# Selective-scan kernel: the gating product issued one scan later at group borders, and a fourth buffer for quads of C

## The chip, the cores and the metric

The kernel runs on one core of a Trainium2 chip. The metric is the device time of one execution in microseconds (us); the time of a kernel is the median of several runs. One execution was also taken by the hardware profiler, and the views shown below are of that execution.

The core's engines are named as the profile names them: PE (TensorE, with PEld for its weight loads), DVE (VectorE), ACT (ScalarE), POOL (GpSimd) and SP (SyncE, which here only issues DMAs). Each engine works its own instructions strictly in the order in which the program issued them; engines wait for each other on semaphores.

## The reference

An image batch `x` of shape (2, 96, 128, 128) goes through two layers. Layer 0 has the work that matters here, four selective scans ("mamba") over the 16384 positions of an image, one for each direction of reading it:

```python
def step(h, t):
    dt_t, u_t, B_t, C_t = t
    dA = jnp.exp(dt_t[:, :, None] * A)
    h = dA * h + dt_t[:, :, None] * B_t[:, None, :] * u_t[:, :, None]
    y = jnp.einsum('bds,bs->bd', h, C_t)
    return (h, y)
...
y = ys.transpose(1, 0, 2) + Dp * xc
y = y * jax.nn.silu(z)
return y @ outp_w.T
```

There are 192 inner channels a direction and 16 states a channel. `xc`, `z`, `dt`, `B` and `C` come from small projections of the normalized input. After the four scans come a fused projection with a residual, a quantized feed-forward layer, a 3x3 convolution and a second feed-forward layer. Everything is float32 outside the feed-forward layers.

## The kernel before

For each of the two images there are three stages: `normalize` (L155), `mamba` (L185) and `ffn_and_conv` (L492). Only `mamba` is touched.

**Steps, groups, units.** Two directions are computed together, and their 2 x 192 channels fill three groups of 128 partitions (`g` = 0, 1, 2). A pair of directions takes 32 steps of T = 512 positions. There are two pairs an image, so 64 steps an image and 128 in all. Within a step the work is cut into 24 units: a unit is a group and two of its 16 states, `units = [(g, s) ...]` (L384). In this text a unit is named by its place in the step, 0 to 23; units 0 to 7 are group 0, 8 to 15 group 1, 16 to 23 group 2. Groups begin at units 0, 8 and 16.

**What a unit costs each engine.**
- SP fetches B and C. Both lie in DRAM as rows, and `row_tile` (L329) broadcasts a quad (four states, two units) over the partitions: one DMA of 1024 KB. The quads of B go round `B_AHEAD + 1` = 4 buffers, the quads of C round `C_AHEAD + 1` = 3.
- POOL multiplies a quad of B by dt*u in place (`b_part`, L339, 128x2048), then adds what the states carry over from the step before (L342, L343).
- ACT makes the decay exp(dt*A) into PSUM (`decay`, L349, two of 128x512). There are three such PSUM buffers.
- DVE runs the recurrence (`scan`, L353), two scans of 512 positions, and then multiplies the result by C in place of C (L441, 128x1024). For the units in `BY_POOL`, which are 0, 4, 8, 12, 16 and 20, POOL makes this product instead (`by_pool`, L360).
- ACT copies the last state aside (L442).
- PE sums the products over the states by matmuls with the identity (`sums`, L357) into the PSUM tile `y`. There is one `y` buffer. A group's `y` is opened by a matmul of the skip term (L448).

When a group is complete, DVE multiplies `y` by silu(z): the gate (`gated`, L364, 128x512). Only then can L448 of the next group open `y` again.

**Order.** `in_order` (L150) fixes the order in which every engine gets its instructions to the program's own. The loop at L469 goes over all units `k`: fetch B for unit k+6 and run `b_part` for unit k+2 (even k), prologue work of the next step that falls due (`issue(k, 0)`), first scan of unit k, then `behind(k - 1)`, the decay of unit k+2, the second scan of unit k, fetch of C for unit k+4 (even k), and the rest that falls due (`issue(k, 1)`). `behind(k - 1)` is what follows unit k-1's scans: the product with C, the copy of the state, at a group's begin the gate of the group before and L448, and the sums. Where POOL makes the product of unit k, it is issued in iteration k+1 and its sums on PE in iteration k+3.

So at a group's begin DVE gets: the first scan of unit k, the gate of the group that ended with unit k-2, the second scan of unit k. In a step these gates fall on iterations 9 (for group 0), 17 (for group 1) and 1 of the next step (for group 2).

**Prologue.** The next step's projections are spread over the units by `prologue` (L214) with a table of due times (L308 to L323): two convolutions of eight matmul pairs or matmuls at iterations 1, 5 and 9 (L211), z at 7, 18 and 21, rows of B and C at 12 (L266), dt at 14 to 16 (L284, L289), softplus at 17 (L293), dt*u on POOL at 19, 27 and 29 (L298). They share one PSUM tile, `misc`. The output projection of a group (`project`, L372 and L374) is due four units after its end and uses `misc` too.

**Buffers.** A DMA into a buffer waits on SP until the last reader of the old contents is done. For a quad of C the last reader is PE (L357); with a POOL unit in it that is three iterations after the unit.

Of the kernel before, what the change touches and what calls it, by code (L numbers as in the profile page):

```python
# [30 lines left out]
PAIRS = ((0, 2), (1, 3))  # L31
NG = 3
B_AHEAD = 3
C_AHEAD = 2
AHEAD = 2
BY_POOL = tuple((g, s) for g in range(3) for s in (0, 8))
BCO = 32
# [4 lines left out]
def tile_metaformer(ctx: ExitStack, tc: tile.TileContext, a: dict, out: bass.AP):  # L42
    nc = tc.nc
# [141 lines left out]
    def mamba(acc, xnr, xnc):  # L185

        with ExitStack() as st:
# [164 lines left out]
            def scan(j, da, b, h):  # L352
                nc.vector.tensor_tensor_scan(h[:, j, :], da[:, j, :], b[:, j, :], 0.0, ALU.mult, ALU.add)  # L353

            def sums(s, y, c):
                for j in range(2):
                    nc.tensor.matmul(y, ident, c[:, j, :], start=False, stop=s + j == S - 1)  # L357
# [4 lines left out]
            def gated(pi, d, g, y):  # L362
                t = d["sz"][:, g, :]
                nc.vector.tensor_tensor(t, y, t, ALU.mult)  # L364
                d["yg"].append(t[:, ::-1] if pi == 1 else t)
# [17 lines left out]
            steps = [(pi, i) for pi in range(2) for i in range(NT)]  # L383
            units = [(g, s) for g in range(NG) for s in range(0, S, 2)]  # L384
            nu = len(units)
            total = nu * len(steps)
            state = [{} for _ in steps]
            todo = {}

            def later(k, where, rank, f, *args):  # L390
                todo.setdefault((k, where), []).append((rank, partial(f, *args)))

            def issue(k, where):
                for _, f in sorted(todo.pop((k, where), ()), key=lambda p: p[0]):
                    f()
# [7 lines left out]
            def prepare(n):  # L403
                if n < len(steps):
                    for m, where, rank, f in prologue(*steps[n], state[n]):
                        k = (n - 1) * nu + m
                        if k < 0:
                            f()
                        else:
                            later(k, where, rank, f)  # L410
# [4 lines left out]
            def fetch(k, n, ahead, m):  # L415
                if k < total:
                    t = row_tile(state[k // nu], *units[k % nu], n, ahead)
                    m[k], m[k + 1] = t[:, 0:2, :], t[:, 2:4, :]
                    if n == 0:
                        quads[k] = t  # L420

            def feed(k):

                if k < total:
                    n = k // nu
                    b_part(steps[n][1], state[n], *units[k % nu], quads.pop(k))

            def feed_decay(k):
                if k < total:
                    n = k // nu  # L430
                    das[k] = decay(steps[n][0], state[n], *units[k % nu])

            ys = {}

            def behind(k):

                n, u = divmod(k, nu)
                (pi, i), d, (g, s) = steps[n], state[n], units[u]
                h, c = hs.pop(k), cs.pop(k)
                if (g, s) not in BY_POOL:  # L440
                    nc.vector.tensor_tensor(c, h, c, ALU.mult)  # L441
                nc.scalar.copy(hst[:, g, s : s + 2], h[:, :, T - 1])  # L442
                if s == 0:
                    if k > 0:
                        pn, pu = divmod(k - 1, nu)
                        gated(steps[pn][0], state[pn], units[pu][0], ys.pop(k - 1))
                    y = ps_y.tile([128, T], F32, name="y")
                    nc.tensor.matmul(y, dmat[:, pi, g, :], d["xc"][:, g, :], start=True, stop=False)  # L448
                else:
                    y = ys.pop(k - 1)  # L450
                ys[k] = y
                if (g, s) in BY_POOL:
                    later(k + 1, 1, True, by_pool, h, c)
                    later(k + 3, 1, True, sums, s, y, c)
                else:
                    sums(s, y, c)
                if k == total - 1:
                    gated(pi, d, g, y)
                if s == S - 2 and g > 0:
                    later(k + 4, 0, True, project, pi, i, d, g)  # L460
                    later(k + 5, 1, False, collect, pi, d, g)

            for m, (n, ahead) in ((bs, (0, B_AHEAD)), (cs, (1, C_AHEAD))):
                for k in range(ahead):
# [4 lines left out]
            for k in range(total + 6):  # L469
                n, u = divmod(k, nu)  # L470
                if u == nu - 3:

                    prepare(n + 2)
                if k % 2 == 0:
                    fetch(k + 2 * B_AHEAD, 0, B_AHEAD, bs)
                    feed(k + AHEAD)
                issue(k, 0)
                if k < total:
                    (g, s) = units[u]
                    da, b = das.pop(k), bs.pop(k)  # L480
                    hs[k] = b if (g, s) in BY_POOL else da
                    scan(0, da, b, hs[k])
                if 0 < k <= total:
                    behind(k - 1)
                feed_decay(k + AHEAD)
                if k < total:
                    scan(1, da, b, hs[k])
                if k % 2 == 0:
                    fetch(k + 2 * C_AHEAD, 1, C_AHEAD, cs)
                issue(k, 1)  # L490
# [101 lines left out]
    for b in range(NB):  # L592
        xnr = dpool.tile([C, L], F32, name="xnr")
        xnc = dpool.tile([C, L], F32, name="xnc")
        normalize(b, acc, xnr, xnc)
        mamba(acc, xnr, xnc)
        ffn_and_conv(b, acc)
# [71 lines left out]
```

## Time and profile before

| what | value |
|---|---|
| median of 3 runs | 11550.82 us |
| lowest to highest | 11549.54 to 11551.47 us |
| the profiled execution's own time | 11556.77 us |
| its span, first to last instruction | 11555.0 us |
| busy in the stretch 6100 to 10900 us (4800 us of `mamba`) | DVE 4639.98, POOL 4506.79, PE 4366.64, ACT 3387.67 us |
| DMA in that stretch | mean busy share 0.86 of 16 engines, 331 GB/s |
| TensorE's mean granted clock | 0.989 over the span, 1.00 in that stretch |

How to read it: the span is what lies between the first and last instruction, and the execution's own time is 1.8 us more. Busy is the time in which an engine executes; waits on semaphores are not in it. `mamba` is the two long stretches of the span, one for each image, some 500 to 5200 us and 6000 to 10950 us with their beginnings. A group's row in the profile ends with the idle time of its engine just before it and with who ended that idle time. In a timeline, a row gives start, duration, engine, line, and in brackets the idle time before it.

### The profile page before, as it was taken

How to read it: one execution, taken by the hardware profiler on the slowest of the kernel's cores; microseconds unless marked ns; L12 is line 12 of the kernel's file. 1: busy time of each engine (PE TensorE's matmuls, PEld its weight loads, DVE VectorE, ACT ScalarE, POOL GpSimd, SP SyncE). 2: the span in 40 equal slices, each digit the busy share in tenths (PEclk: the TensorE clock that was granted, in tenths of full speed). 3: DMA queues.
4: the chain of work that ended last, by engine and by line, in shares of the span. 5: the costliest groups of instructions: out<-in, count | busy, mean ns of one | idle time of the engine just before them, and what ended most of it. 6: DMA issues, size and time to landing. Idle time of an engine off the chain costs nothing. (4 is left out here: it accounts for less than half of the span.)

```text
span 11555.0 us, 94102 instructions
## 1 busy us (share of the span) xinstructions
PE 10435.0 (90%) x24208; PEld 3971.4 (34%) x24208; DVE 10421.6 (90%) x10127; ACT 7901.7 (68%) x13564; POOL 9672.3 (84%) x4700
## 2 busy tenths in 40 slices
PE   7999999999999999989989999999999999999899
PEld 2333333333333333333323333333333333333333
DVE  6999999999999999994469999999999999999944
ACT  6767767677677677665567677677676776776655
POOL 5999999999999999991159999999999999999911
PEclk8999999999999999999989999999999999999999
DMA  7888888888888888880068888888888888888800
GB/s 263 335 329 333 333 332 332 330 331 333 329 332 333 330 331 333 329 322 19 26 243 334 328 331 334 330 333 333 333 331 329 332 332 329 331 333 329 319 13 13
DMA packets 540755, 3416.96 MB, mean 296 GB/s; under 512 B 67532, under 2 KB 68652, under 8 KB 143832
## 3 DMA queue, kind: packets, MB, share of 16 engines
q1 hardware_dynamic: 539960, 3410.16, 76.8%
q8 instruction: 196, 3.21, 0.1%
q14 instruction: 343, 2.81, 0.1%
q0 software_dynamic: 256, 0.79, 0.0%
HBM read 3289.04 MB, written 54.53 MB: 289 GB/s over the span
## 5 line engine op out<-in xcount | busy, mean ns | idle before, releaser
L339 POOL TENSOR_TENSOR row<-dtu,row 128x2048 f32<-128x2048 f32 x1536 | 6948.9, 4524 | 283.3 <-DMA row<-bcd 281.6
L357 PE MATMUL y<-row,ident 128*128 128x512 f32 x12288 | 5690.6, 603 | 700.0 <-DVE row L441 699.9
L353 DVE TENSOR_TENSOR_SCAN da<-da,row 128x512 f32<-128x512 f32 x4608 | 5456.9, 1214 | 38.9 <-ACT da L349 5.2
L349 ACT ACTIVATE da<-dt,amat 128x512 f32<-128x512 f32 x6144 | 4246.9, 691 | 170.2
L357 PEld LDWEIGHTS y<-row,ident 128*128 128x128 f32 x12288 | 2256.8, 190 | 4008.4 <-issue 2243.5
L441 DVE TENSOR_TENSOR row<-da,row 128x1024 f32<-128x1024 f32 x2304 | 2776.7, 1205 | 70.2 <-DMA row<-bcd 70.0
L442 ACT COPY hst<-da 128x2 f32<-128x2 f32 x2304 | 368.9, 160 | 2652.2 <-DVE row L441 2649.3
L360 POOL TENSOR_TENSOR row<-row,row 128x1024 f32<-128x1024 f32 x768 | 1807.4, 2353 | 223.0 <-DVE row L353 147.5
L353 DVE TENSOR_TENSOR_SCAN row<-da,row 128x512 f32<-128x512 f32 x1536 | 1852.4, 1206 | 91.9 <-POOL row L339 84.1
L211 PE MATMUL misc<-xa,inx 96*64 96x512 f32 (+1 forms) x2048 | 946.1, 605 | 50.0 <-ACT mix L239 26.8
L211 PE MATMUL misc<-xb,inx 96*64 96x512 f32 (+1 forms) x2048 | 952.3, 608 | 33.6 <-ACT hst L442 24.2
L564 POOL TENSOR_TENSOR acc<-acc,y 96x512 f32<-96x512 f32 x128 | 147.4, 1151 | 991.5 <-DVE y L563 991.5
L298 POOL TENSOR_TENSOR dtu<-dt,xc 128x512 f32<-128x512 f32 x384 | 487.4, 1269 | 106.0 <-DMA xb<-xnc 99.8
L576 PE MATMUL pc<-pad,kw 96*96 96x512 f32 x1152 | 566.4, 593 | 0.0
L211 PEld LDWEIGHTS misc<-xa,inx 96*64 96x64 f32 (+1 forms) x2048 | 327.3, 165 | 581.2 <-issue 438.0
L448 PE MATMUL y<-xc,dmat 128*128 128x512 f32 x768 | 419.5, 628 | 103.6 <-DVE sz L364 103.6
L374 PE MATMUL misc<-sz,gmat 128*96 128x512 f32 x1024 | 484.1, 595 | 0.0
L284 PE MATMUL misc<-rows,dtw 12*128 12x512 f32 x768 | 434.3, 645 | 50.6 <-ACT dt L289 37.9
L364 DVE TENSOR_TENSOR sz<-y,sz 128x512 f32<-128x512 f32 x384 | 264.6, 689 | 229.5 <-PE y L357 198.0
L136 DVE TENSOR_TENSOR xq<-xm,rs 96x512 fp8e5<-96x512 f32 x128 | 87.9, 687 | 392.2 <-ACT rs L132 392.2
L211 PEld LDWEIGHTS misc<-xb,inx 96*64 96x64 f32 (+1 forms) x2048 | 316.5, 164 | 361.9 <-issue 214.1
L372 PE MATMUL misc<-acc,ident 96*96 96x512 f32 x512 | 387.6, 842 | 57.3 <-ACT sz L247 53.8
(76 smaller groups left out, 7449.9 us busy)
## 6 DMA issues: line engine op xcount, KB each, us to landing
row<-bcd SPq DMA_DIRECT2D x3072, 1024.0 KB, 7.4
xc<-mix SPq DMA_DIRECT2D x256, 128.0 KB, 5.4
sz<-mix SPq DMA_DIRECT2D x256, 128.0 KB, 8.9
xa<-xnr SPq DMA_DIRECT2D x124, 193.1 KB, 8.6
xb<-xnc SPq DMA_DIRECT2D x124, 193.1 KB, 8.7
bcd<-rows SPq DMA_DIRECT2D x128, 128.0 KB, 9.5
acc<-in_x_dram SPq DMA_DIRECT2D x16, 768.0 KB, 5.7
xnr<-xn SPq DMA_DIRECT2D x16, 768.0 KB, 4.3
```

The costliest lines, as they stand in the source:

```text
L211: nc.tensor.matmul(ps[rows, :], w(PAIRS[pi][d], k, lo, hi), src[d][:, k : k + T], **se)
L284: nc.tensor.matmul(d["ps"], w, d["rows"][0 : 2 * RK, :], start=True, stop=True)
L298: nc.gpsimd.tensor_tensor(dtu, d["dt"][:, g, :], d["xc"][:, g, :], ALU.mult)
L339: nc.gpsimd.tensor_tensor(b, d["dtu"][g][:, None, :].broadcast_to((128, 4, T)), b, ALU.mult)
L349: nc.scalar.activation(da[:, j, :], d["dt"][:, g, :], AF.Exp, scale=amat[:, pi, g, s + j : s + j + 1])
L353: nc.vector.tensor_tensor_scan(h[:, j, :], da[:, j, :], b[:, j, :], 0.0, ALU.mult, ALU.add)
L357: nc.tensor.matmul(y, ident, c[:, j, :], start=False, stop=s + j == S - 1)
L360: nc.gpsimd.tensor_tensor(c, h, c, ALU.mult)
L374: nc.tensor.matmul(d["po"], gmat[:, pi, 2 * g - 2 + k, :], d["yg"][g - 1 + k], start=False, stop=k == 1)
L441: nc.vector.tensor_tensor(c, h, c, ALU.mult)
L448: nc.tensor.matmul(y, dmat[:, pi, g, :], d["xc"][:, g, :], start=True, stop=False)
L576: nc.tensor.matmul(pc, kw[:, t, :], rows, start=t == 0, stop=t == 8)
```

## The change

Three edits.

1. `gate_before` holds the gate that stood in `behind`, and `begins(k)` tells whether unit k begins a group and has its product made by POOL (units 0, 8 and 16, which is every group's begin). Where unit k-1 begins a group, the whole of `behind(k - 1)` is issued after the second scan of unit k, not between its two scans. With it move the copy of the state on ACT (now behind the decay of unit k+2) and, on PE, the skip term's matmul L448; the order within PE, POOL and SP stays.
2. `C_AHEAD` goes from 2 to 3: C is fetched for unit k+6 where it was unit k+4, and the quads of C go round four buffers of 8 KB a partition.
3. The space for it: the scratch for DMAs that GpSimd issues is set to 4096.

```diff
-C_AHEAD = 2
+C_AHEAD = 3
...
+            def gate_before(k):
+                pn, pu = divmod(k - 1, nu)
+                gated(steps[pn][0], state[pn], units[pu][0], ys.pop(k - 1))
+
+            def begins(k):
+                return 0 <= k < total and units[k % nu][1] == 0 and units[k % nu] in BY_POOL
...
                 if s == 0:
                     if k > 0:
-                        pn, pu = divmod(k - 1, nu)
-                        gated(steps[pn][0], state[pn], units[pu][0], ys.pop(k - 1))
+                        gate_before(k)
...
-                if 0 < k <= total:
+                if 0 < k <= total and not begins(k - 1):
                     behind(k - 1)
                 feed_decay(k + AHEAD)
                 if k < total:
                     scan(1, da, b, hs[k])
+                if begins(k - 1):
+                    behind(k - 1)
...
-    nc = bacc.Bacc("TRN2", target_bir_lowering=False, num_devices=1)
+    nc = bacc.Bacc("TRN2", target_bir_lowering=False, num_devices=1, dynamic_dma_scratch_size=4096)
```

## The prediction

> **What bounds it now.** I read the busy times by stage first: in 6100 to 10900 us DVE is busy 4639.98 of 4800 us (97%), POOL 94%, PE 91%. So DVE carries the mamba stage, and the groups tell what its idle time is made of.
>
> ```profile
> L339 POOL TENSOR_TENSOR row<-dtu,row 128x2048 f32<-128x2048 f32 x1536 | 6948.9, 4524 | 283.3 <-DMA row<-bcd 281.6
> L441 DVE TENSOR_TENSOR row<-da,row 128x1024 f32<-128x1024 f32 x2304 | 2776.7, 1205 | 70.2 <-DMA row<-bcd 70.0
> L364 DVE TENSOR_TENSOR sz<-y,sz 128x512 f32<-128x512 f32 x384 | 264.6, 689 | 229.5 <-PE y L357 198.0
> ```
>
> The two waits that the change aims at are 229.5 us before the gates and 70.2 us before DVE's products: 300 us together. The first row is the warning: POOL too waits, for quads of B.
>
> Second, DVE's timeline over one step (gate to gate 79.1 us, 2015.52 to 2094.62). Columns: start, duration.
>
> ```profile
> 2013.17 1.21 DVE L353 TENSOR_TENSOR_SCAN da<-da,row 128x512 f32<-128x512 f32 x1
> 2015.52 0.69 DVE L364 TENSOR_TENSOR sz<-y,sz 128x512 f32<-128x512 f32 x1 [1.15 <-PE y L357]
> ...
> 2040.94 0.69 DVE L364 TENSOR_TENSOR sz<-y,sz 128x512 f32<-128x512 f32 x1
> ...
> 2060.21 1.22 DVE L441 TENSOR_TENSOR row<-da,row 128x1024 f32<-128x1024 f32 x1 [0.50 <-DMA row<-bcd]
> 2061.35 1.22 DVE L353 TENSOR_TENSOR_SCAN da<-da,row 128x512 f32<-128x512 f32 x1
> 2062.48 1.20 DVE L353 TENSOR_TENSOR_SCAN row<-da,row 128x512 f32<-128x512 f32 x1
> ...
> 2067.72 0.69 DVE L364 TENSOR_TENSOR sz<-y,sz 128x512 f32<-128x512 f32 x1 [0.67 <-PE y L357]
> ```
>
> The gate of group 1 waits 1.15, that of group 2 not at all, that of group 0 0.67, and one product waits 0.50 for C. A scan starts 1.12 after the one before (2061.35 to 2062.48), so one scan put ahead of a gate covers 1.12.
>
> Third, POOL in the same step: how far ahead of DVE is it?
>
> ```profile
> 2035.62 4.52 POOL L339 TENSOR_TENSOR row<-dtu,row 128x2048 f32<-128x2048 f32 x1 [0.78 <-DMA row<-bcd]
> ...
> 2057.43 4.53 POOL L339 TENSOR_TENSOR row<-dtu,row 128x2048 f32<-128x2048 f32 x1
> 2061.91 0.23 POOL L342 TENSOR_TENSOR enter<-enter,hst 128x16 f32<-128x16 f32 x1
> 2062.22 0.20 POOL L343 TENSOR_TENSOR row<-row,enter 128x4 f32<-128x4 f32 x1
> ```
>
> L343 at 2062.22 finishes the B of unit 8 at 2062.42, and the scan of unit 8 starts at 2062.48. In this step POOL is 0.06 ahead. Over the trace's 118 full steps it is 0.43 ahead on average there, never under 0.03 (the hand-over) and under 1.39; at every other unit the median is 1.06 or more. **That place decides the case.**
>
> **Where POOL's lateness at unit 8 comes from.** I follow it back. From 2035.62 POOL has no gap until 2062.42 but one of 0.40: 26.8 us. At 2035.62 it waited for the quad of B for unit 2. SP issued that at 2028.70 and it landed 6.9 later (2035.56). It stood behind a quad of C issued at 2028.33, for which SP had waited 8.7 us on PE's sums. Those came late because PE's projection L372 at 2022.05 had waited for ACT's copy L247 to free `misc`, and ACT had had no gap since DVE's product of unit 15:
>
> ```profile
> 2012.16 0.16 ACT L442 COPY hst<-da 128x2 f32<-128x2 f32 x1 [1.14 <-DVE row L441]
> 2012.35 1.42 ACT L349 ACTIVATE da<-dt,amat 128x512 f32<-128x512 f32 x2
> 2013.70 0.67 ACT L289 ACTIVATE dt<-misc,dtb 128x512 f32<-128x512 f32 x1
> ...
> 2015.78 1.28 ACT L293 ACT_TABLE_LOAD   x1
> ...
> 2021.42 0.58 ACT L247 COPY sz<-misc 128x512 f32<-128x512 f32 x1
> ```
>
> So a second chain runs beside DVE: product of unit 15 (ends 2012.12), ACT to 2022.00, PE to 2028.3, DMA to 2035.56, POOL to 2062.42, scan of unit 8. It begins ahead of the gate of group 1 and ends behind the C wait. Nothing on it is touched.
>
> **The change, part by part.**
>
> *Gate of group 1 (iteration 17).* Now: scan, 1.15 idle, gate, scan. After: scan, scan, gate. PE's sums still end at 2015.50; the second scan fills 2014.29 to 2015.50, and what follows runs some 1.1 earlier. L448 starts after the gate as now (2016.27). The copy of the state goes behind one decay on ACT, which has the same work up to the softplus.
>
> *The fourth C buffer.* Before, C for unit k+4 goes, in iteration k, into the third buffer back, that of units k-2 and k-1. After, C for unit k+6 goes into the fourth back: the same units. So SP waits for the same sums at the same moment, and B behind it is no earlier; only C is needed 2 units (6.7 us) later. The 0.50 wait goes (70.2 us over the kernel, 0.63 in the steps' mean), and POOL's waits for B do not.
>
> *Both meet the second chain.* DVE would reach unit 8 some 1.12 + 0.63 = 1.75 earlier, and POOL is ready only 0.43 - 0.03 = 0.40 earlier. So from both edits I count **0.40 a step**; the other 1.35 turns into a new wait of DVE's scan for POOL (L353 on L343; 7.1 us now).
>
> *Gate of group 0 (iteration 9).* It lies behind unit 8. Group 1's gate takes 1.15 x 126 = 145 of the 229.5 us, which leaves 85 / 126 = 0.67 a step. PE ends this group's sums by 2067.7; the second scan would end, from 2062.48, at about 2068.1, so the gate waits no more. From there to the product of unit 15 DVE has 0.67 to 0.72 less; I take **0.70**. What is late next? POOL at unit 12: median 1.06 ahead, tenth percentile 0.58, so that now and then 0.1 is lost. ACT at unit 10 ends its decay 0.10 to 0.35 ahead of the scan, but its run of work there begins with the product that loses the C wait, 1 us earlier or more.
>
> *Gate of group 2 (iteration 1).* It doesn't wait now and comes 1.12 later relative to the scans. Behind it L448 waits on PE, and behind L448 the sums. The cover is the convolution ahead of L448 in PE's queue (eight L211 pairs, 2040.82 to 2044.41), against a shifted gate done by 2042.7. Cost nothing; uncovered, up to 1.12 a step. Group 0's L448 has the convolution until 2071.36 as cover.
>
> *The smaller scratch.* POOL issues four DMAs in all (L226, 1.1 us to issue, 5.8 or less to land), at the stages' beginnings. Between nothing and 4 x 5.8 = 23 us; I take nothing, as POOL's L298 waits up to 51.3 us there in any case. One more quad of C ahead of the first step: the next DMA landed 2.5 us behind the one before (2033.06, 2035.56), so 0 to 5 us for two stages; taken as 0.
>
> **Sum.** 0.40 + 0.70 = 1.10 us a step, times 126 steps (the two first ones are bound by the start) = 139 us. From the profiled execution, 11556.8 - 139 = 11418; its time is 6.0 over the median of the runs, so 11550.8 - 139 = **11412**.
>
> [...]
>
> **Rivals.**
>
> 1. *The gaps go entirely.* If the chain to unit 8 gives way (if quads of B come sooner once PE's sums are earlier), all goes but the 0.11 a step of group 1's gate beyond 1.12: 300 - 14 = 286, so 11265. For it: POOL's 283.3 us of DMA waits and 223.0 ahead of L360 are idle time. Against it: those ahead of unit 8 sit at a landing tied to ACT and PE, not to DVE's scans. Chance 0.20, from 180 us of gain up.
> 2. *The new wait eats the gate too.* POOL at unit 12, or ACT at unit 10, holds DVE as soon as it is 0.7 early: 0.40 x 126 = 50, so 11501. Chance 0.13, for a gain of 23 to 95.
> 3. *Slower: the covers on PE are gone.* Group 0's and 2's L448 come 1.12 later each if the convolutions don't hide them; every sum behind them, the release of C and the B behind it in SP's queue come later, and POOL at unit 8 has no room. 2 x 1.12 x 126 = 282 lost, 139 won: 11694. It decides from 1.10 a step. Against it: PE runs without a gap from 2047.3 to 2074.1, behind both gates. Chance 0.10.
> 4. *No change*, within 23 us: POOL's chain is itself slower by what the gate wins. Chance 0.05.
>
> **Chances and range.** The forecast holds 95 to 180 us of gain, chance 0.52. Faster by over 0.2% (23 us, about what this measurement can tell from no change): 0.52 + 0.20 + 0.13 = 0.85; within 0.05; slower 0.10. For 8 in 10 the range reaches from the full gain, 11260, to the small one, 11505; what lies outside is the slower case, no change and a sliver below.
>
> **What would show it.** Right: L364's idle falls from 229.5 to under 30, L441's wait for DMA vanishes, and DVE's scan waits for POOL's L343 with about 1.3 a step, 170 us, at unit 8; POOL's waits for B stay at 250 or more; a step takes 78.0. Wrong: no such wait for L343 (rival 1), waits for ACT's decay or L343 at units 10 to 14 (rival 2), L448 and L357 on PE waiting for L364 more than 104 us (rival 3). What would upset it most is a DMA that lands sooner or later than in this trace: POOL's chain hangs on it.

## The result, and the profile after

| | before | after |
|---|---|---|
| median of 4 runs each | 11550.18 us | 11812.88 us |
| lowest to highest | 11547.0 to 11551.47 | 11794.68 to 11834.05 us |
| span of the profiled execution | 11555.0 us | 11809.1 us |
| mean granted TensorE clock | 0.989 | 0.969 |

The changed kernel takes 1.0228 times the time of the one before, 95% interval 1.0211 to 1.0246: 263 us slower, where 139 us faster was forecast. A step takes 81.29 us where it took 79.20. (L441, L442 and L448 of before are now L448, L449 and L454.)

The groups of instructions of the changed kernel; behind the bar are busy time, mean ns of one, idle time just before them and what ended most of it:

```profile
L339 POOL TENSOR_TENSOR row<-dtu,row 128x2048 f32<-128x2048 f32 x1536 | 6946.9, 4523 | 388.2 <-DMA row<-bcd 384.3
L353 DVE TENSOR_TENSOR_SCAN da<-da,row 128x512 f32<-128x512 f32 x4608 | 5500.0, 1216 | 223.9 <-ACT da L349 186.9
L448 DVE TENSOR_TENSOR row<-da,row 128x1024 f32<-128x1024 f32 x2304 | 2770.3, 1202 | 0.1
L353 DVE TENSOR_TENSOR_SCAN row<-da,row 128x512 f32<-128x512 f32 x1536 | 1852.1, 1206 | 240.1 <-POOL row L343 148.9
L364 DVE TENSOR_TENSOR sz<-y,sz 128x512 f32<-128x512 f32 x384 | 259.9, 677 | 193.2 <-PE y L357 192.9
```

Read row by row: the products wait for C no longer (70.2 before, 0.1 now). The scans wait 148.9 for POOL's L343, which is the new wait that the prediction named. But two rows are not as forecast. The scans wait 186.9 for ACT's decays; the same row of the kernel before has

```profile
L353 DVE TENSOR_TENSOR_SCAN da<-da,row 128x512 f32<-128x512 f32 x4608 | 5456.9, 1214 | 38.9 <-ACT da L349 5.2
```

And the gates still wait 193.2, where under 30 was forecast.

**The wait for the decay** is at the same unit in every step but the first ones. DVE's timeline from one unit 8 (start, duration, idle before in brackets):

```profile
2033.12 1.22 DVE L353 TENSOR_TENSOR_SCAN row<-da,row 128x512 f32<-128x512 f32 x1 [0.54 <-POOL row L343]
...
2036.51 2.47 DVE L353 TENSOR_TENSOR_SCAN da<-da,row 128x512 f32<-128x512 f32 x2
2038.89 0.67 DVE L364 TENSOR_TENSOR sz<-y,sz 128x512 f32<-128x512 f32 x1
...
2041.73 2.33 DVE L353 TENSOR_TENSOR_SCAN da<-da,row 128x512 f32<-128x512 f32 x2
...
2048.45 1.21 DVE L353 TENSOR_TENSOR_SCAN row<-da,row 128x512 f32<-128x512 f32 x1
2051.14 3.61 DVE L353 TENSOR_TENSOR_SCAN da<-da,row 128x512 f32<-128x512 f32 x3 [1.48 <-ACT da L349]
```

2048.45 is the second scan of unit 12 (POOL makes its product, so its scans write to `row`). The first of unit 13 then stands still for 1.48. ACT in the same place:

```profile
2049.70 1.41 ACT L349 ACTIVATE da<-dt,amat 128x512 f32<-128x512 f32 x2 [1.37 <-DVE row L353]
...
2053.87 0.57 ACT L272 COPY rows<-misc 96x512 f32<-96x512 f32 x1
```

ACT wants to write the decay of unit 13 and waits until DVE has scanned unit 12; then DVE waits while ACT writes. That is what two neighbouring units in one buffer look like. The kernel's text did not touch the decays, so I read which of the three PSUM buffers each unit's decay was given in the built programs. With the buffers numbered as they first come, from unit 0: 0, 1, 2, 0, 1, 2, 0, 1, 2, 0, 2, 1, 0, 2, 1 before; 0, 1, 2, 0, 1, 2, 0, 1, 2, 0, 2, 1, **0, 0**, 2 after. Units 12 and 13 share one, in 124 of the 128 steps.

**The clock.** ACT's copy of the rows (L272) comes late in turn, and PE, which needs them for dt, has a gap. PE's timeline in one step and in the next:

```profile
2051.34 1.88 PE L357 MATMUL y<-row,ident 128*128 128x512 f32 x4
2054.50 1.12 PE L284 MATMUL misc<-rows,dtw 12*128 12x512 f32 x2 [1.27 <-ACT rows L272]
2055.93 1.98 PE L357 MATMUL y<-row,ident 128*128 128x512 f32 x4 [0.31 <-DVE row L448]
...
2134.67 1.12 PE L284 MATMUL misc<-rows,dtw 12*128 12x512 f32 x2 [1.27 <-ACT rows L272]
2136.10 3.65 PE L357 MATMUL y<-row,ident 128*128 128x512 f32 x4 [0.31 <-DVE row L448]
```

The same four matmuls behind the same two gaps take 1.98 in the first step and 3.65 in the second. The windows of the second step show what is different: the clock (busy time and count of each engine, then the granted clock, DMA share and GB/s):

```profile
core 0: us, PE busy (x) PEld busy (x) DVE busy (x) ACT busy (x) POOL busy (x), PEclk, DMA share, GB/s
...
2134.00:2136.00 2.00, 1.12 (x2) 0.29 (x2) 2.00 (x3) 0.62 (x2) 2.00 (x1) 1.00 1.26 426
2136.00:2139.50 3.50, 3.40 (x4) 1.18 (x4) 3.50 (x5) 2.20 (x5) 3.42 (x4) 0.51 0.87 309
2139.50:2143.00 3.50, 3.50 (x9) 1.36 (x9) 3.50 (x4) 2.26 (x6) 2.80 (x2) 1.00 0.70 289
```

The granted clock is halved for 3.4 us here and for 3.4 to 10.2 us in other steps, in all drops but one 44 to 46 us after the gate of group 2 starts. Behind it PE's sums of group 1 end late, and the gate of group 1 waits for them. The first line is this gate in the step with the full clock, the second in the one with half:

```profile
2066.02 0.67 DVE L364 TENSOR_TENSOR sz<-y,sz 128x512 f32<-128x512 f32 x1
...
2147.44 0.69 DVE L364 TENSOR_TENSOR sz<-y,sz 128x512 f32<-128x512 f32 x1 [1.15 <-PE y L357]
```

Of 121 steps that I counted in the trace, 81 have such a stretch: 82.22 us each, with a mean wait of 2.27 at that gate. The 40 others take 79.31, with no wait there.

### The profile page after: what moved, and what is told of

It reads as the page before. It is cut to its first block, busy times and chain, and to the rows that moved or that the text cites. A ratio compares the mean times of both kernels' runs of the same rounds, so it can differ in the third digit from the quotient of the medians.

```text
span 11809.1 us, 93354 instructions
## 1 busy us (share of the span) xinstructions
PE 10642.9 (90%) x24208; PEld 4047.3 (34%) x24208; DVE 10447.2 (88%) x10127; ACT 7876.3 (67%) x13564; POOL 9666.1 (82%) x4700
## 4 chain that ended last, share of the span: by engine, by line
DVE 41%; PE 26%; issue 13%; ACT 11%; DMA 4%; POOL 4%; SPq 0%; DVEq 0%; POOLq 0%; ACTq 0%
DVE da L353 24%; PE y L357 10%; DVE row L353 8%; DVE row L448 7%; ACT da L349 5%; PE pc L584 4%; POOL row L339 3%; PE misc L211 3%; DMA xa<-xnr 3%; PE misc L284 2%; PE v L128 2%; PE xm L122 2%; DMA row<-bcd 1%; ACT sz L259 1%; ACT L259 1%
## 5 line engine op out<-in xcount | busy, mean ns | idle before, releaser
L339 POOL TENSOR_TENSOR row<-dtu,row 128x2048 f32<-128x2048 f32 x1536 | 6946.9, 4523 | 388.2 <-DMA row<-bcd 384.3
L357 PE MATMUL y<-row,ident 128*128 128x512 f32 x12288 | 5870.7, 618 | 450.6 <-DVE row L448 445.5
L353 DVE TENSOR_TENSOR_SCAN da<-da,row 128x512 f32<-128x512 f32 x4608 | 5500.0, 1216 | 223.9 <-ACT da L349 186.9
L357 PEld LDWEIGHTS y<-row,ident 128*128 128x128 f32 x12288 | 2301.3, 194 | 3872.9 <-issue 2316.1
L448 DVE TENSOR_TENSOR row<-da,row 128x1024 f32<-128x1024 f32 x2304 | 2770.3, 1202 | 0.1
L353 DVE TENSOR_TENSOR_SCAN row<-da,row 128x512 f32<-128x512 f32 x1536 | 1852.1, 1206 | 240.1 <-POOL row L343 148.9
L449 ACT COPY hst<-da 128x2 f32<-128x2 f32 x2304 | 369.4, 160 | 2406.9 <-DVE row L448 2403.7
L284 PE MATMUL misc<-rows,dtw 12*128 12x512 f32 x768 | 479.6, 706 | 179.7 <-ACT rows L272 161.4
L372 PE MATMUL misc<-acc,ident 96*96 96x512 f32 x512 | 385.7, 838 | 204.4 <-ACT sz L247 119.4
L454 PE MATMUL y<-xc,dmat 128*128 128x512 f32 x768 | 420.2, 629 | 110.2 <-DVE sz L364 110.2
L364 DVE TENSOR_TENSOR sz<-y,sz 128x512 f32<-128x512 f32 x384 | 259.9, 677 | 193.2 <-PE y L357 192.9
```

The lines of the kernel that those rows point to most:

```text
L284: nc.tensor.matmul(d["ps"], w, d["rows"][0 : 2 * RK, :], start=True, stop=True)
L339: nc.gpsimd.tensor_tensor(b, d["dtu"][g][:, None, :].broadcast_to((128, 4, T)), b, ALU.mult)
```

## The experiments

The theory from the traces (S): the fourth C buffer, by the space that it takes, changed which PSUM buffer a unit's decay gets (that it is not the space shows in early_late_noring, below); units 12 and 13 share one, DVE and ACT wait for each other, and PE's gap behind it costs half the clock. The rival theories: the later gate does it (its copy of the state, or its L448 on PE); or the C transfers, fetched earlier, disturb the quads of B, for which POOL waits 388.2 us where it waited 283.3.

**after_ring.** The change, with the decays' buffers strictly in turn.

```diff
-            def decay(pi, d, g, s):
+            def decay(pi, d, g, s, k):
-                da = ps_w.tile([128, 2, T], F32, name="da")
+                da = ps_w.tile([128, 2, T], F32, name=f"da{k % 3}", bufs=1)
```

> The changed kernel, with the three PSUM buffers of the decays given out strictly in turn (unit k into buffer k mod 3). Theory S (shared buffer): in the changed kernel the allocator gives units 12 and 13 of a step the same buffer, so that the decay of unit 13 waits for both scans of unit 12; that costs DVE 1.34 us a step at unit 13, delays ACT and the dt chain behind it, lets PE idle until its clock is halved, and makes the gate of group 1 wait. Then with buffers in turn ACT's wait in front of unit 13 falls from 187 us to under 40, the clock returns to 0.985 or more, and the time is that of the forecast, 11380 to 11440. Theory L (late matmul): L454 and the sums behind it, issued one scan later, are what makes PE late; then nothing changes: 11780 to 11840.

Measured: 11464.58 us, 0.9924 of before (0.9909 to 0.9939). The clock is back at 0.989, and the scans' rows read

```profile
L353 DVE TENSOR_TENSOR_SCAN da<-da,row 128x512 f32<-128x512 f32 x4608 | 5501.0, 1216 | 55.9 <-POOL row L343 3.8
...
L353 DVE TENSOR_TENSOR_SCAN row<-da,row 128x512 f32<-128x512 f32 x1536 | 1853.2, 1207 | 260.0 <-POOL row L343 169.7
```

The wait for ACT is gone, and that for POOL's L343 is 169.7, where 170 was forecast. Only the buffers of the decays differ from the changed kernel, and 348 us go with them (11812.88 - 11464.58). That points to the shared buffer as the cause of the loss (before_shared, below, tries it alone). But the time missed the expectation too, by 25 us: a second fault, of size, to which I come back.

**gate_only** and **c_only.** One half of the change each; nothing done about the decays.

```diff
-C_AHEAD = 3
+C_AHEAD = 2
...
-    nc = bacc.Bacc("TRN2", target_bir_lowering=False, num_devices=1, dynamic_dma_scratch_size=4096)
+    nc = bacc.Bacc("TRN2", target_bir_lowering=False, num_devices=1)
```

The diff above makes gate_only from the changed kernel; c_only is the kernel before with the two `+` and `-` lines the other way round.

> Only the later gate: C_AHEAD stays 2 and the scratch is as before. In this build units 12 and 13 have different buffers. Theory S: no loss at unit 13; the gate of group 0 wins 0.70 a step and the 0.40 that GpSimd is early at unit 8 are won too, though VectorE's wait for C may take their place: 11400 to 11450. Theory L: the late gate is the loss, so 11750 or more.

> Only the fourth buffer for C with the smaller scratch; the gate stands between the two scans as before. In this build units 12 and 13 share a buffer. Theory S: 0.40 a step won at unit 8, 1.34 lost at unit 13, and PE's clock falls too: 11650 to 11830. Theory L: no gate was moved, so nothing is lost: 11490 to 11550.

Measured: gate_only 11456.31 us, 0.9915 (0.99 to 0.993), clock 0.989, 6 us above its range; c_only 11955.98 us, 1.0349 (1.0332 to 1.0366), clock 0.966. In the built programs, c_only has units 12 and 13 in one buffer and gate_only has the buffers of the kernel before. So the later gate is innocent, and the rival that blames it falls; the loss comes with the other half, the fourth C buffer and C fetched two units earlier. c_only loses more than the changed kernel and more than expected. Its gates tell where: half the clock in 120 of 121 steps, and a gate with one scan less ahead of it.

```profile
L364 DVE TENSOR_TENSOR sz<-y,sz 128x512 f32<-128x512 f32 x384 | 264.0, 688 | 495.1 <-PE y L357 494.3
```

**before_shared.** The kernel before, with the shared buffer alone: the decays go in turn, except that unit 13 takes unit 12's.

```diff
-            def decay(pi, d, g, s):
+            def decay(pi, d, g, s, k):
-                da = ps_w.tile([128, 2, T], F32, name="da")
+                da = ps_w.tile([128, 2, T], F32, name=f"da{(k - (k + 11) // 24) % 3}", bufs=1)
```

> The kernel before, unchanged in order and C buffers, with the decays' buffers given out in turn except that unit 13 takes unit 12's. Theory S: the shared buffer alone makes it slower, by 1.34 us a step or more: 11700 to 11850, with a clock under 0.98. Theory L: within 0.5% of the kernel before, 11500 to 11610.

Measured: 11965.38 us, 1.0357 (1.0342 to 1.0372), clock 0.965. With no fourth C buffer, no changed scratch and the old gate, it does all that c_only does:

```profile
L353 DVE TENSOR_TENSOR_SCAN da<-da,row 128x512 f32<-128x512 f32 x4608 | 5458.7, 1214 | 213.1 <-ACT da L349 194.1
...
L364 DVE TENSOR_TENSOR sz<-y,sz 128x512 f32<-128x512 f32 x384 | 264.1, 688 | 470.7 <-PE y L357 432.4
```

The third theory, the transfers of C, is not needed; c_ring, below, has these transfers and loses nothing. The size was again underrated: 115 of 121 steps have the half clock (82.53 us, against 81.02 for the others).

**before_ring** and **c_ring.** The controls: the kernel before with its decays in turn, and the changed kernel in turn with the old gate (`f"da{k % 3}", bufs=1` as in after_ring).

> The kernel before with the decays' buffers strictly in turn, nothing else. Both theories: within 0.2% of the kernel before, 11527 to 11573, as its own order of buffers has no two neighbouring units in one buffer. A gain or loss here would have to be taken off the other kernels with buffers in turn.

> Only the fourth buffer for C as in the change (fetched for unit k+6), the decays' buffers in turn, the gate as before. Theory B: VectorE's wait for C, 0.63 a step, goes, and 0.3 of it comes back as a wait for GpSimd at unit 8: 11490 to 11525. If the shared buffer was not the whole loss of the fourth buffer, over 11600.

Measured: before_ring 11558.52 us, c_ring 11557.71 us, both 1.0005 (0.9995 to 1.0014). The turn by itself is worth nothing. The fourth C buffer, without the shared buffer, is worth nothing either, though it does what it is for; here c_ring missed its range of 11490 to 11525. In c_ring the product with C waits for nothing, but the gates, which waited 229.5, now wait 267.5, and the scans wait 46.1 for POOL's L343, where it was 7.1:

```profile
L441 DVE TENSOR_TENSOR row<-da,row 128x1024 f32<-128x1024 f32 x2304 | 2773.9, 1204 | 0.1
...
L353 DVE TENSOR_TENSOR_SCAN row<-da,row 128x512 f32<-128x512 f32 x1536 | 1853.6, 1207 | 135.4 <-POOL row L339 88.1 <-POOL row L343 46.1
...
L364 DVE TENSOR_TENSOR sz<-y,sz 128x512 f32<-128x512 f32 x384 | 264.6, 689 | 267.5 <-PE y L357 265.3
```

About half of the wait for C became a wait at unit 8 for POOL. The other half became a wait of the gate of group 0 for PE: its mean went from 0.69 to 1.01.

**after_fill2** and **after_fill4.** How much of the loss is the clock? The changed kernel with the shared buffer left as it is, and PE's gap filled by two, or four, matmuls of a zero matrix ahead of the first matmul for dt. They add zeros to `y`.

```diff
+    zero = cpool.tile([128, 128], F32, name="zero")
+    nc.vector.memset(zero, 0.0)
...
+                    if g == 0 and not first:
+                        for _ in range(2):
+                            nc.tensor.matmul(ys[max(ys)], zero, d["xc"][:, 0, :], start=False, stop=False)
```

> The changed kernel with the shared buffer left in, plus two matmuls of a zero matrix a step that add nothing to y; they stand on PE ahead of the first dt matmul, where PE waits 1.27 us for ACT's rows. Theory K (clock): the most of the changed kernel's loss is PE's clock, which is granted at half for 3.4 us and more behind that gap in two steps of three; those steps take 82.2 us, the others 79.3. If PE has work in the gap the clock stays whole and all steps take about 79.3 to 79.6: 11560 to 11620, mean clock 0.985 or more. Theory W (waits): the longer chain from the shared buffer through ACT to PE is the loss by itself; then more work on PE changes nothing or costs: 11790 to 11900.

> [...] Theory K: the clock stays whole too, but the dt matmuls come about 1.7 us later than with two, which the gate of group 1 feels: 11600 to 11760. Theory W: 11800 to 11950.

Measured: after_fill2 11628.25 us, 1.0068 (1.0053 to 1.0083), clock 0.989, half clock in one step, and DVE's wait of 1.48 at unit 13 still there; after_fill4 11784.65 us, 1.0202 (1.0187 to 1.0218), clock 0.989. Two more matmuls a step for PE make the kernel 185 us faster (11812.88 - 11628.25). By this at least 185 of the 348 us are the clock's; 164 remain to the waits at the shared buffer and to the two extra matmuls a step, which this run does not part. The steps of the changed kernel itself divide it alike: (82.22 - 79.31) x 81/121 x 126 = 245 for the clock and (79.31 - 78.53) x 126 = 98 for the waits, 78.53 being after_ring's step; after_fill2 pays for its own matmuls, so its share of the clock is the lower. Four matmuls are too many: the full clock holds, but the gate of group 1 waits 1.29 a step for PE. Both came out above their expectations, after_fill2 by 8 us. No run shows the 1.7 us by which after_fill4's expectation has the dt matmuls later than with two: in after_fill2 the matmuls of zeros keep PE busy for 0.47 each (236.8 us for 504), so two more are some 0.94.

**early_late_gate** and **early_old_gate.** Does the second chain yield if B is issued sooner? The quads of C have four buffers but are fetched for unit k+4 as before; their DMA then waits for sums that lie two units further back, and B behind it in SP's queue is no longer held up by them. The decays go in turn. One has the later gate, one the old.

```diff
-C_AHEAD = 3
+C_AHEAD = 2
...
-                t = gen.tile([128, 4, T], F32, name=f"row{k}", bufs=ahead + 1)
+                t = gen.tile([128, 4, T], F32, name=f"row{k}", bufs=4)
```

> The later gate, the decays' buffers in turn, four buffers for quads of C, but C fetched for unit k+4 as before, so that SyncE waits for sums that are two units older. Theory B (order of SyncE): what keeps VectorE from the full gain is the second chain: B for unit 2 stands in SyncE's queue behind a quad of C that waits for PE's sums. With the older sums B comes early, the scan's wait for GpSimd at unit 8 goes, and with it all gate waits: 77.0 us a step, 11250 to 11330. Theory D (transfers): the quads of B are late because the DMA engines can't bring them sooner; then the time stays at that of the later gate with buffers in turn, 11440 to 11480.

> The same four buffers with C fetched for unit k+4 and the decays' buffers in turn, but the gate between the two scans as before. Theory B: only the wait for C (0.63 a step) and the few waits for GpSimd (0.10) go, the gates' 1.9 a step stay: 11440 to 11480. Theory D: nothing or little: 11520 to 11560.

Measured: early_late_gate 11336.92 us, 0.9813 (0.9799 to 0.9828); early_old_gate 11541.18 us, 0.999 (0.9981 to 1.0). The first is just above its range: ACT's decay at unit 10 now ends last, 0.45 a step. The second missed its range of 11440 to 11480 entirely: with the old gate all that DVE gains at unit 8 is lost at the gate of group 0, which waits 1.37.

```profile
L364 DVE TENSOR_TENSOR sz<-y,sz 128x512 f32<-128x512 f32 x384 | 264.6, 689 | 311.4 <-PE y L357 311.4
```

**early_late_noring.** early_late_gate with the decays left to the allocator (`name="da"`); no neighbours share a buffer in this program. It differs from the changed kernel in one thing, C fetched for unit k+4 and not for unit k+6.

> The fastest kernel so far (later gate, four buffers for C with C fetched for unit k+4) with the decays' buffers left to the allocator. In this build units 12 and 13 have different buffers. If only a shared buffer matters, and not the turn as such, the time is that of the one with buffers in turn, 11315 to 11360; if the turn itself wins something, over 11380.

Measured: 11317.45 us, 0.9798 (0.9782 to 0.9815), clock 0.990, a step 77.33: the fastest, 234 us ahead of the kernel before, and in its range. So the buffers in turn are not needed, and the reason in theory S falls: this program has the same four C buffers and the same scratch as the changed kernel, so it is not the space that put units 12 and 13 into one buffer. It goes with fetching C two units further ahead. POOL's wait for DMAs, 283.3 in the kernel before, is nearly gone:

```profile
L339 POOL TENSOR_TENSOR row<-dtu,row 128x2048 f32<-128x2048 f32 x1536 | 6951.0, 4526 | 8.6 <-DMA row<-bcd 8.6
```

And SP, the DMAs' queue, waits for PE's sums 2444.7 us. The first of these lines is the kernel before's, the second early_late_noring's (total, times, longest):

```profile
SPq L335 <- PE y L357: 6879.4, 1404, 11.1
```

```profile
SPq L335 <- PE y L357: 2444.7, 768, 5.0
```

So the same fourth buffer goes with a loss of 402 us where two neighbours came to share a PSUM buffer (c_only, against 11554.1 in its comparison), wins nothing where C is fetched further ahead, and helps to win 234 where it lets the old contents go sooner.

## Why the prediction was wrong

The sign came out wrong by one step of the prediction, the size by two others. These are means over the steps in us, counted from the end of the product of unit 15, where the second chain begins.

| | before | after_ring | gate_only | c_ring | early_late_gate | after |
|---|---|---|---|---|---|---|
| PE starts L372 | 9.93 | 9.95 | 9.95 | 9.93 | 9.95 | 11.50 |
| POOL starts on unit 2's B | 23.50 | 23.75 | 23.54 | 23.54 | 21.57 | 25.17 |
| POOL ends L339 for unit 8 | 49.62 | 49.86 | 49.68 | 49.69 | 47.94 | 51.28 |
| DVE starts unit 8 | 50.49 | 50.35 | 50.20 | 50.21 | 48.77 | 51.77 |
| from there to the next product of unit 15 | 28.71 | 28.19 | 28.26 | 29.01 | 28.70 | 29.53 |
| step | 79.20 | 78.53 | 78.46 | 79.22 | 77.47 | 81.29 |

- **The step that failed: "The fourth C buffer."** It priced the wait for C, SP's order and, beside it, the smaller scratch, "I take nothing". What the edit does to buffers that its text leaves alone it put at nothing without a reason. With C fetched for unit k+6, units 12 and 13 came to share a PSUM buffer: that cost DVE 1.57 a step at unit 13 beyond its bare instructions (0.24 before), and half of PE's clock for some us in two steps of three, 348 us together. No rival had either; the slower one put its price on L448.
- **The clock** was read as 1.00 in the stretch and taken for a constant of the kernel. It went with PE's gap ahead of the step's first L284: PE is idle there for 0.08 us in the mean of the kernel before and for 1.29 in the changed kernel, and with two matmuls in that gap 1 step has the half clock, where 81 had it (after_fill2).
- **"Both meet the second chain"** was right as a mechanism. c_ring's wait for C, 0.63 a step, is gone and nothing is won. The new wait for L343 is 1.35 a step in after_ring (1.3 forecast). And with POOL out of the way, DVE does come sooner: in early_late_gate, where POOL ends 1.68 sooner, unit 8 starts 1.72 sooner, close to the 1.75 that the prediction had for DVE alone. The term of **0.40** was too large, though: 0.14 in after_ring and 0.29 in gate_only. DVE did come nearer to POOL, from 0.87 to 0.49 behind L339's end (L342 and L343 lie between), 0.38 of the forecast 0.40; but POOL was itself 0.24 later in after_ring. The sentence "Nothing on it is touched" was too strong: POOL starts on unit 2's B 0.25 later there, and 0.04 in gate_only and in c_ring. It takes both halves of the change together; why was not traced.
- **Gate of group 0: 0.70** a step measured 0.52 in after_ring and 0.45 in gate_only (28.71 less 28.19 and 28.26). The gate's wait is gone as forecast, but 0.12 of it was given back. The two scans ahead of a shifted gate are of one unit, without another instruction between them; the timeline above has two such at 2036.51 that take 2.47, against 2.33 at 2041.73 for two of different units. That is at three places in a step. The other 0.06 to 0.13 was not traced.
- Sum, with the decays in turn: 79.20 - 78.53 = 0.67 a step, times 126 = 84 us, of 139 forecast; the runs show 89.5 (11554.1 before in that comparison, less 11464.58).
- **Gate of group 1** waits no more in the steps with the full clock, as forecast. **Gate of group 2: cost nothing** held but for the 0.12. **The smaller scratch** as a space for DMAs costs nothing that shows: c_ring has it and equals the kernel before (1.0005).
- **Rivals.** 1, the chain gives way: not in the change, but early_late_gate shows that it can, 214 us of the 286 named. (The 0.11 a step in it is not what its lines give: 1.15 less 1.12 is 0.03, so 4 us in place of 14.) 2, the new wait eats the gate: not at unit 12; DVE waits for ACT's decays 48.2 us in early_late_gate and 12.6 in gate_only. 3, the covers on PE are gone: refuted, since gate_only has the same later L448, with PE's wait there the same 110.2 us as in the changed kernel, and is faster. (PE's stretch "without a gap" has one of 0.21 us, at 2067.82.) 4, no change: true of the C buffer alone.

Open: why the allocator gave two neighbours one buffer once C was fetched two units further ahead. Which buffer each decay gets was read from the built programs; the allocator's rule was not looked into. Open too: why 40 of 121 steps kept the full clock behind the same gaps; no run shows it.

## What to carry to other kernels

When a change adds a buffer, fetches further ahead or moves an instruction, read in the built program which buffer every tile of the tight pools gets, before and after: a text that is unchanged does not say that its buffers are. The granted clock can be lost with such a change, too (a mean of 0.989 before, 0.969 after): compare it step by step, and not as a mean alone. A wait removed from the busiest engine was won here only as far as the next engine was ahead at that place (in c_ring the wait for C, 0.63 a step, is gone, and the time is 1.0005 of before), and that slack has to be taken along the other engine's own chain. Here an extra buffer helped to win 234 us where it let the transfers queued behind it start (early_late_noring), and won nothing where it fetched its own data further ahead (c_ring).

## What the runs showed of the hardware

**Half the clock behind short gaps of PE.** The window above has a granted clock of 0.51 right behind gaps of 1.27 and 0.31 us. In the 3.4 us ahead of a drop, PE was idle for a median of 1.43 us in the changed kernel and 1.58 in before_shared, in single gaps of 1.6 at most but for one of 3.7. Filling one place with two matmuls of zeros brought the steps with half clock from 81 to 1 (after_fill2); the kernel before has none and after_ring 5.

The gaps alone do not tell which step loses the clock: the two steps of the changed kernel above have the same 1.27 and 0.31 us, with the same pair of L284 of 1.12 between, and one kept the full clock where the other lost it. What decides between them was not shown: no run varied the length or the place of the gaps by themselves.

**Scans.** Two scans of the same unit directly after one another take 2.47 us together, and two of different units 2.33: 0.14 here, and 0.12 from start to start (1.24, the mean of the 382 pairs ahead of a gate in the changed kernel, against 1.12). Why was not tried.
